# Block 3's cross-attention: groups of two heads by 2048 keys, a lead of three key tiles, first keys loaded beside block 2

## The chip, the cores and the metric

The kernel runs on one core of one Trainium2 chip. The metric is the device time of one execution in microseconds. The program is a four-block perceiver in one launch: each block has a cross-attention to a long context, a self-attention and a feed-forward part, with two batches of 256 query rows and 4096 context rows of 256 values each.

## The reference, cut to what matters

The part that is changed is the cross-attention of block 3: ordinary masked softmax attention of 16 heads of 16 values.

```python
def _L3_xattn_ref(hidden_states, context, attention_mask, q_w, q_b, k_w, k_b, v_w, v_b):
    B, LQ, LK, D = (4, 512, 512, 256)
    H = 16
    HD = D // H
    ...
    q = _split_heads(hidden_states @ q_w.T + q_b)
    k = _split_heads(context @ k_w.T + k_b)
    v = _split_heads(context @ v_w.T + v_b)
    scores = jnp.einsum('bhqd,bhkd->bhqk', q, k) / jnp.sqrt(jnp.float32(HD))
    mask = (attention_mask > 0)[:, None, None, :]
    scores = jnp.where(mask, -jnp.inf, scores)
    probs = jax.nn.softmax(scores, axis=-1)
    ctx = jnp.einsum('bhqk,bhkd->bhqd', probs, v)
    ...
x = x + _L3_xattn_ref(_layernorm(x, axis=-1), ctx_1024, mask_BxS2_ik0, ...)
x = x + _L3_attn_ref(...)
x = x + _L3_ffn_ref(...)
```

In the data x has 2 batches of 256 rows and the context 2 batches of 4096 rows. Block 2 before it ends with a self-attention (`_L2_attn_ref`) and a mixture of eight experts with a shared one (`_L2_ffn_ref`).

## The kernel before, in words

Two "lanes" of tiles, a and x, allocate from the two ends of SBUF and PSUM, so that work of batch 0 and of batch 1, or of two stages, can stand beside each other. Python emits instructions in program order; the framework then places each on its engine's queue by a simulated time line, and each engine runs its queue in order. All loads and stores are issued from SP's queue.

Block 3's keys and values don't depend on x. They are projected earlier, beside blocks 0 to 2 (`prep`, lines 864 to 885), and written to DRAM: keys as a rounded part `kh_d` and its remainder `kl_d`, in units of 512 keys, values as `v_d`, with a column of ones behind each head's 16 values, so that the same product gives the sum of the exponents. `x3_queries` (line 1325) writes the queries of a batch to `q_d` in the same two parts.

`l3_xattn` (line 1333) is a generator; `run` (line 1889) drives it, and where it yields `1, None` the feed-forward part of block 2 for batch 1 (`af(2, 1)`, which is `l2_ffn` and `x3_queries`) is emitted, so that the two run beside each other. The work is cut into groups of four heads (`GRP`), 8 groups in all, and each group into `N_C` = 4 key tiles of 1024 keys: 32 tiles. A key tile `k` is [128, 4 heads, 512]: two halves of 64 partitions, each half 512 keys, and in a half the rows r, r+4, r+8, ... hold the three products of the split (queries high and low against keys high and low), row 3 the mask, row 7 the shift. One contraction over 64 rows so gives the full score, with mask and, later, minus the row's maximum added.

A tile passes twice. `max_steps` (line 1348) loads the tile, multiplies 128 queries by 2 x 512 keys into a tile "f" of two PSUM banks (L1374) and takes maxima on VectorE (L1376), eight steps a tile. When a group's four tiles are through, the maxima are combined (L1380), split in two parts, transposed on PE (`shift_rows`, L557), copied by VectorE (L559) and written by two DMAs into row 7 of the queries. Then `exponents` (line 1385) multiplies again, keys as the stationary operand (L1397), and ScalarE takes exponentials of 128x512 out of a score bank (L1398), two a step, eight steps a tile. `finish` (line 1403) multiplies them by the values (`mh_values`, L580), the four heads of a group in the four 32-row strips of the bank `acc`. At a group's end VectorE copies `acc` (`mh_finish`, L598), PE transposes it (L606), VectorE divides (L609, L610) and POOL adds x and the bias (L1421, L1422).

The maxima run ahead of the exponents by `n_c + LEAD` = 5 tiles. After the first five tiles, `advance` puts one maximum step ahead of each exponent step, and `tie` keeps PE's instructions in that order. Seven key tiles form a ring (`RING`); the rows of ones in them come from a memset by POOL (L1296), once a tile of the ring.

PSUM has eight banks here: two tiles "f" of two banks, one score bank "s" of lane x, two banks "mm" and one "acc" of lane a. Score tiles rotate over "s", "mm", "mm"; the two banks "mm" are also those of block 2's feed-forward part of batch 1, which is emitted first. Small products (L557, L606) take a tile "f". The first four key tiles and the query tiles lie in a pool `early` of lane a; the others in a pool `late` that opens when block 2's attention of batch 1 (`l2_attn(x, 1, ...)`, line 1886) has been emitted.

## Time and profile before

The time is 1528.7 us, median of three executions (1523.4 to 1534.8). The profiled execution took 1525.8 us.

| | PE | DVE | ACT | POOL |
|---|---|---|---|---|
| busy in the span of 1524.0 us | 1363.6 us (89%) | 1109.5 us (73%) | 890.6 us (58%) | 521.0 us (34%) |
| busy from 872 to 960 us | 63.6 | 71.8 | 17.1 | 19.3 |
| busy from 960 to 1241 us | 275.2 | 270.8 | 234.5 | 6.2 |
| busy from 1241 to 1289 us | 46.7 | 3.6 | 43.4 | 1.3 |

In the views of the profile, PE is the matrix engine and PEld its weight loads, DVE is VectorE, ACT ScalarE, POOL GpSimd, SP the engine that issues DMAs; a name with a q is the engine's sequencer. A row of the table of groups gives line, engine, operation, output <- input, shapes and count, then busy time and the mean ns of one, then the idle time of the engine just before these instructions and what ended it. Tile names carry the lane as their first letter: `xf` is the tile "f" of lane x, `amm` a bank "mm" of lane a. A row of a timeline gives start and length in us, engine, line, operation and, in brackets, the idle time before it. PE's busy times are modelled and overlap.

Block 3's cross-attention lies between 872 us, when its first reduction starts, and 1288.6 us, when its last division ends. Block 3's self-attention and experts follow.

### The profile page before, as it was taken

What the parts mean: (1) busy time and instruction counts of PE and PEld (TensorE: products, weight loads), DVE (VectorE), ACT (ScalarE), POOL (GpSimd) and SP (SyncE); (2) the same over time, 40 slices, a digit from 0 to 9 for tenths busy, and PEclk for the clock granted to TensorE, in tenths of its full rate; (3) what the DMA queues carried; (4) which work ended last, traced back from release to release, by engine and by line L of the source; (5) the groups of instructions that cost most, each with busy time, mean ns of one, the idle gap of its engine ahead of it and who ended that gap; (6) DMA issues with size and microseconds to landing.
All of it is one profiled execution on the core that took longest, in us unless ns stands there. A gap on an engine that the chain in (4) does not pass through costs nothing.

```text
span 1524.0 us, 29340 instructions
## 1 busy us (share of the span) xinstructions
PE 1363.6 (89%) x11278; PEld 1117.7 (73%) x11278; DVE 1109.5 (73%) x1879; ACT 890.6 (58%) x1668; POOL 521.0 (34%) x389
## 2 busy tenths in 40 slices
PE   7999888978999999999998677999999999888688
PEld 6898778968998998998897346555555555774587
DVE  6899756437467878885577597899999961575775
ACT  5676555637776655764663312788888897233343
POOL 6755344336355554674235503000000001520230
PEclk9999999979999999999999758899999999996799
DMA  8744064566455566445633642333333312200361
GB/s 295 232 154 134 29 185 156 182 177 200 163 184 175 165 183 210 148 152 176 187 98 102 203 153 79 99 126 117 107 126 106 108 53 66 102 1 3 130 244 56
DMA packets 125143, 212.00 MB, mean 139 GB/s; under 512 B 12840, under 2 KB 89240, under 8 KB 121480
## 3 DMA queue, kind: packets, MB, share of 16 engines
q1 hardware_dynamic: 125004, 210.13, 43.4%
q8 instruction: 89, 1.46, 0.4%
q14 instruction: 50, 0.41, 0.1%
HBM read 181.32 MB, written 28.61 MB: 138 GB/s over the span
## 4 chain that ended last, share of the span: by engine, by line
PE 38%; DVE 24%; DMA 5%; ACT 4%; POOL 4%; issue 3%; SPq 1%; POOLq 0%; DVEq 0%; ACTq 0%
DVE xpm L1376 15%; PE amm L412 9%; PE xmm L412 6%; PE xs L412 4%; PE xpr L412 3%; PE xacc L580 3%; DMA awr<-in_w 2%; PE amm L1397 2%; POOL aw L405 2%; PE xf L1374 1%; PE xmm L784 1%; PE amm L1761 1%; ACT aw L403 1%; PE amm L580 1%; DVE aw L406 1%
## 5 line engine op out<-in xcount | busy, mean ns | idle before, releaser
L1376 DVE TENSOR_REDUCE xpm<-xf 128x2 f32<-128x1024 f32 x256 | 309.8, 1226 | 11.5 <-PE xf L1374 10.1
L1398 ACT ACTIVATE xp<-amm 128x512 f32<-128x512 f32 x342 | 194.5, 595 | 33.7 <-PE amm L1397 16.6
L403 ACT CAST aw<-awr 128x1024 fp32r<-128x1024 f32 (+1 forms) x112 | 114.2, 1021 | 109.8 <-DMA awr<-in_w 55.5
L412 PE MATMUL xmm<-xvx,xpT 128*128 128x256 f32 x1152 | 167.5, 292 | 5.0 <-DVE xpT L787 2.2
L405 POOL TENSOR_TENSOR aw<-awr,aw 128x1024 fp32r<-128x1024 f32 (+1 forms) x53 | 126.2, 2383 | 130.2 <-ACT aw L403 127.8
L412 PE MATMUL xs<-xkx,xqkT 128*128 128x256 f32 x1152 | 163.5, 286 | 1.0 <-ACT xqkT L397 0.6
L734 POOL TENSOR_TENSOR xvx<-xraw,xvx 128x512 fp32r<-128x512 f32 x96 | 132.2, 1392 | 88.8 <-ACT xvx L732 82.9
L580 PE MATMUL xacc<-xp,xv 128*17 128x256 f32 x2048 | 161.1, 387 | 0.9 <-DVE xot L598 0.9
L1374 PE MATMUL xf<-xk,xq 64*128 64x512 f32 x512 | 135.9, 529 | 20.6 <-DVE xpm L1376 13.2
L412 PEld LDWEIGHTS xmm<-xvx,xpT 128*128 128x128 f32 x1152 | 147.9, 193 | 8.6 <-issue 3.6
L412 PEld LDWEIGHTS xs<-xkx,xqkT 128*128 128x128 f32 x1152 | 149.0, 193 | 2.9 <-issue 0.8
L1374 PEld LDWEIGHTS xf<-xk,xq 64*128 64x128 f32 x512 | 51.4, 196 | 125.4 <-issue 86.6
L406 DVE TENSOR_TENSOR aw<-awr,aw 128x1024 fp32r<-128x1024 f32 (+1 forms) x59 | 83.2, 1411 | 64.8 <-ACT aw L403 64.5
L1397 PE MATMUL amm<-xq,xk 64*128 64x256 f32 x684 | 112.5, 294 | 2.7 <-DVE aqT L401 2.6
L1421 POOL TENSOR_TENSOR ax<-ax,ax 128x128 f32<-128x128 f32 x8 | 3.7, 457 | 325.2 <-DVE ax L610 325.2
L1398 ACT ACTIVATE xp<-xs 128x512 f32<-128x512 f32 x170 | 101.1, 595 | 16.5 <-PE amm L1397 11.3
L412 PE MATMUL amm<-axnT,aw 128*128 128x256 f32 x636 | 100.0, 315 | 12.0 <-ACT axnT L403 5.0
L1397 PEld LDWEIGHTS amm<-xq,xk 64*128 64x128 f32 x684 | 95.3, 187 | 17.2 <-issue 12.8
L412 PEld LDWEIGHTS amm<-axnT,aw 128*128 128x128 f32 x636 | 92.0, 219 | 19.8 <-ACT axnT L403 6.8
L412 PE MATMUL amm<-ah,aw 128*128 128x256 f32 x768 | 99.1, 285 | 6.0 <-ACT au L1009 3.1
L734 POOL TENSOR_TENSOR xkx<-xraw,xkx 128x512 fp32r<-128x512 f32 x48 | 73.5, 1531 | 86.6 <-ACT xkx L732 84.2
L412 PEld LDWEIGHTS amm<-ah,aw 128*128 128x128 f32 x768 | 94.3, 190 | 8.5 <-ACT au L1009 3.7
(593 smaller groups left out, 2852.2 us busy)
## 6 DMA issues: line engine op xcount, KB each, us to landing
awr<-in_w SPq DMA_DIRECT2D x105, 512.0 KB
xraw<-in_ctxT SPq DMA_DIRECT2D x108, 256.0 KB
xraw<-in_ctx SPq DMA_DIRECT2D x96, 256.0 KB
xk<-akh_d SPq DMA_DIRECT2D x64, 256.0 KB
av_d<-xkvv SPq DMA_DIRECT2D x16, 544.0 KB
xv<-av_d SPq DMA_DIRECT2D x32, 272.0 KB
akh_d<-xkvk SPq DMA_DIRECT2D x32, 256.0 KB
akl_d<-xkvk SPq DMA_DIRECT2D x32, 256.0 KB
```

Of the source, the lines that this page charges most:

```text
L403: nc.scalar.copy(dst.h, src)
L405: return lo.tensor_tensor(dst.l, src, dst.h.bitcast(F32), ALU.subtract)
L406: return nc.vector.tensor_sub(dst.l, src, dst.h)
L412: tie(self.nc.tensor.matmul(out, lhsT=x, rhs=y, start=start and i == 0, stop=stop and i == 2))
L580: inst = self.nc.tensor.matmul(acc[STRIP * j : STRIP * j + v(j).shape[1], :S], lhsT=v(j), rhs=p[:, j, :], start=start, stop=stop)
L734: nc.gpsimd.tensor_tensor(x.l, r, x.h.bitcast(F32), ALU.subtract)
L784: tie(nc.tensor.transpose(pst[:, t * P : (t + 1) * P], p[:, t * P : (t + 1) * P], self.eye))
L1374: tie(nc.tensor.matmul(both[:, h * 512 : (h + 1) * 512], lhsT=q4[rows, j, t * P : (t + 1) * P], rhs=k4[rows, j, :], start=True, stop=True))
L1376: nc.vector.tensor_reduce(at, both.rearrange("p (h n) -> p h n", h=2), axis=AX.X, op=ALU.max)
L1397: tie(nc.tensor.matmul(ps[h][:, j, :], lhsT=ks[c][rows, a + j, s * P : (s + 1) * P], rhs=q4[rows, a + j, :], start=True, stop=True))
L1398: exps = [nc.scalar.activation(p[:, h, a : a + 2, :], ps[h], AF.Exp, scale=0.25) for h in range(2)]
L1761: nc.tensor.matmul(ps[:, f, :], lhsT=w1[half][:, c, f * P : (f + 1) * P], rhs=buf[:, c, e * cap : (e + 1) * cap], start=c == 0, stop=c == 1)
```

## The change

- A group is two heads (`N_G` = 8 groups a batch), a key tile [128, 2 heads, 1024 keys a half], 2048 keys: `N_C` = 2 tiles a group, still 32 tiles of the same bytes. `prep`, `masks`, `x3_queries` and the DRAM tensors are laid out for it. In `acc` the four strips now hold two heads times two halves of the keys, and a product with two identities on top of each other (`fold`) adds the halves while it transposes.
- The lead is `AHEAD` = 3 tiles, the ring 5, the query sets 4.
- `load_keys` is split from `max_steps`. The loads of the first three tiles are emitted before `next(l3)` returns, ahead of block 2's feed-forward part of batch 1; `early` is now a pool of lane x that opens after the cross-attentions of blocks 0 to 2 have closed theirs, and block 2's attention of batch 1 has weight pools of its own and two instead of four "p" buffers.
- Rows of ones and the mask of the first five tiles come by DMA from a tensor `mo_d`, and the memsets are gone.
- The copy of the shift rows and the copy of `acc` are made by ScalarE.
- PSUM: lane a has one bank "mm", one "s", one "acc". Scores rotate over the two "s", and over "mm" too from tile 4 on (`ALL`). Small products take a score bank instead of a tile "f".

```diff
-    def shift_rows(self, mp, nm, qs, step=1):
+    def shift_rows(self, mp, nm, qs, step=1, copy=None):
...
-            nc.vector.tensor_copy(sh, ps[: 2 * n, :S])
+            (copy or nc.vector.tensor_copy)(sh, ps[: 2 * n, :S])
...
-    def score(self):
+    def score_bank(self):
         self.score_turn = (self.score_turn + 1) % len(self.score_tags)
         lane, tag = self.score_tags[self.score_turn]
-        return lane.t(lane.ps, [P, 512], tag).rearrange("p (a n) -> p a n", a=2)
+        return lane.t(lane.ps, [P, 512], tag)
...
-    N_C = L // 1024
+    N_G, KEYS = HEADS // 2, 1024
+    N_C = L // (2 * KEYS)
...
-    RING = 7
-    Q_SETS = 3
-    LEAD = 1
+    RING = 5
+    Q_SETS = 4
+    ALL = 4
+    AHEAD = N_C + 1
...
-            x = tile(f"k{at}", 512)
-            nc.gpsimd.memset(x.bitcast(F32), 1.0)
-            self.x3_k.append(x)
+            self.x3_k.append(tile(f"k{at}", self.KEYS))
...
+        def load_keys(at):
+            b, g, c, i = place(at)
+            q2, k2 = self.x3_tiles(at)
+            if c == 0:
+                state[i] = q2, k.t(self.early, [P, 2, 2, 4 * n_c], "pm", bufs=2), []
+            g2, u2 = slice(2 * g, 2 * g + 2), slice(2 * c, 2 * c + 2)
+            for r, src in ((0, self.kh_d), (1, self.kh_d), (2, self.kl_d)):
+                nc.sync.dma_start(k2[r :: self.PARTS].bitcast(F32), src[b, u2, :, g2, :].rearrange("u d j n -> (u d) j n"))
+            if at < self.RING:
+                nc.sync.dma_start(k2[self.MASK :: self.PARTS].bitcast(F32), self.mo_d[u2].rearrange("u d j n -> (u d) j n"))
+            else:
+                nc.sync.dma_start(k2[self.MASK :: self.HALF].bitcast(F32), self.mk_d[b, u2])
+            state[i][2].append(k2)
...
+                for r, part in enumerate(k.QUERIES):
+                    src = self.q_d[b, part, :, 2 * g : 2 * g + 2, :].unsqueeze(0).to_broadcast([2, HD, 2, S])
+                    nc.sync.dma_start(q2[r :: self.PARTS].bitcast(F32), src)
...
-            for j in range(GRP):
+            for j in range(2):
                 for t in range(2):
+                    for u in range(2):
+                        both = self.x3_find()
...
-                rest = k.shift_rows(self.early, nm, [(q4, h * self.HALF + self.SHIFT) for h in range(2)], self.PARTS)
+                rest = k.shift_rows(self.early, nm, [(q2, h * self.HALF + self.SHIFT) for h in range(2)], self.PARTS, copy=nc.scalar.copy)
...
-                rest = k.mh_finish(g, acc, out[b])
-                later.append([self.LATER, lambda: finished(rest, b, g)])
+                turn = k.ots[i % 2]
+                nc.scalar.copy(turn, acc[:, :S])
+                later.append([self.LATER, lambda: finished(turn, b, g)])
...
+            ps = k.mm()
+            for t in range(2):
+                tie(nc.tensor.matmul(ps[:, 64 * t : 64 * t + 64], lhsT=oT[:, t * P : (t + 1) * P], rhs=fold, start=True, stop=True))
+            ps = ps[:, :P].rearrange("p (t j r) -> p t j r", t=2, j=2)
+            ri = k.t(k.sm, [P, 2, 2], "x3_ri")
+            nc.vector.reciprocal(ri, ps[:, :, :, HD])
...
-        ahead = n_c + self.LEAD
+        for at in range(self.AHEAD):
+            load_keys(at)
+        yield None
...
-            steps = max_steps(at + ahead) if at + ahead < n else iter(())
-            for s in range(4):
+            if at == self.ALL:
+                k.score_tags.append((self.a, "mm"))
+            if at + self.AHEAD < n:
+                load_keys(at + self.AHEAD)
+                steps = max_steps(at + self.AHEAD)
+            for s in range(0, self.KEYS // P, 2):
...
-        k.mm_from = lambda: self.x3_find()[:, :512]
-        k.score_tags = [(k, "s")] + 2 * [(self.a, "mm")]
+        k.mm_from = k.score_bank
+        k.score_tags = [(k, "s"), (self.a, "s")]
...
-        self.v_d = a.dram([B, 4, P, L // 512, 4 * GRP * (HD + 1)], "v_d")
+        self.v_d = a.dram([B, self.N_G, P, L // P, 2 * (HD + 1)], "v_d")
+        self.mo_d = a.dram([n_u, HD, 2, self.KEYS], "mo_d")
...
-                            if n == 2:
-                                self.early = early.enter_context(a.pool("x3e", bufs=2))
...
-                    x.mm_tags = ["mm", "mm", "pr"]
-                    xb[1] = self.l2_attn(x, 1, xb[1])
+                    self.early = early.enter_context(x.pool("x3e", bufs=2))
+                    with x.pool("wraw", bufs=1) as x.wraw, x.pool("w", bufs=2) as x.wp:
+                        x.mm_tags, x.p_bufs = ["mm", "mm", "pr"], 2
+                        xb[1] = self.l2_attn(x, 1, xb[1])
+                    next(l3)
...
-                with ExitStack() as self.x3_psum, self.psum(a, mm=2, acc=1), x.pool("x3", bufs=2) as self.late:
+                with ExitStack() as self.x3_psum, self.psum(a, mm=1, s=1, acc=1), x.pool("x3", bufs=2) as self.late:
```

## The prediction

> **What bounds the kernel now.** I read the page's table of instruction groups first (which row is largest in block 3), then busy time by stretch around that row, then the timelines of POOL, SP and ScalarE at the two ends of the stage. The first view is the table of groups.
>
> ```profile
> L1376 DVE TENSOR_REDUCE xpm<-xf 128x2 f32<-128x1024 f32 x256 | 309.8, 1226 | 11.5 <-PE xf L1374 10.1
> L1398 ACT ACTIVATE xp<-amm 128x512 f32<-128x512 f32 x342 | 194.5, 595 | 33.7 <-PE amm L1397 16.6
> ```
>
> The maxima of block 3 are 256 reductions of 1.226 us on VectorE, 309.8 us in all, with 11.5 us of idle time before them: 32 key tiles of 8 reductions. The exponents are 342 + 170 = 512 ScalarE rows, 16 a tile. The second view is busy time by stretch (columns: window, length, then PE, PEld, DVE, ACT, POOL busy, granted clock, DMA share, GB/s).
>
> ```profile
> 866.00:872.00 6.00, 0.88 (x4) 0.62 (x4) 5.96 (x4) 0.00 (x0) 6.00 (x7) 0.50 0.83 268
> 872.00:900.00 28.00, 18.47 (x57) 8.28 (x54) 26.86 (x42) 1.28 (x3) 3.15 (x3) 0.50 0.61 205
> 900.00:942.50 42.50, 35.20 (x197) 27.07 (x198) 38.45 (x47) 10.29 (x15) 10.73 (x6) 0.82 0.24 82
> 942.50:960.00 17.50, 9.90 (x48) 8.39 (x48) 6.51 (x14) 5.52 (x7) 5.42 (x3) 0.60 0.27 90
> 960.00:1241.00 281.00, 275.20 (x3033) 146.46 (x3031) 270.76 (x262) 234.50 (x432) 6.21 (x13) 0.99 0.35 110
> 1241.00:1289.00 48.00, 46.68 (x504) 22.75 (x502) 3.57 (x13) 43.39 (x81) 1.25 (x3) 1.00 0.12 34
> ```
>
> The stage has three parts. From 872 to 942.5 us VectorE does the 40 reductions of the five tiles of lead beside block 2's FFN of batch 1, and is busy 65.3 of 70.5 us (0.926). From 942.5 to 960 it has little to do (6.5 of 17.5 us): no exponent has run, since the score banks "mm" of lane a belong to that FFN, and the next reductions come only with exponents. From 960 to 1241 it is the limit (270.8 of 281). From 1241 to 1288.6 reductions are over and ScalarE drains five tiles, 43.4 of 48 us busy. The third view is the timeline of POOL and SP at the start, and of ScalarE and SP where exponents begin.
>
> ```profile
> 868.19 5.28 POOL L1296 MEMSET xk<- 128x2048 f32 x3
> 874.56 0.70 POOL L416 TENSOR_TENSOR abn_rs<-abn_ve,amhalf 128x2 f32<-128x2 f32 x1
> ...
> 911.85 11.91 SPq L340 DMA_DIRECT2D awr<-in_w  x3
> 925.04 1.82 SPq L525 DMA_DIRECT2D xq<-xsh_row  x2
> 933.41 14.84 SPq L340 DMA_DIRECT2D awr<-in_w  x4
> ...
> 1081.46 1.09 ACT L1398 ACTIVATE xp<-amm 128x512 f32<-128x512 f32 x2
> 1082.77 0.60 ACT L1398 ACTIVATE xp<-xs 128x512 f32<-128x512 f32 x1 [0.22 <-PE xs L1397]
> 1083.26 1.26 ACT L1398 ACTIVATE xp<-amm 128x512 f32<-128x512 f32 x2
> ```
>
> POOL's memsets of key tiles stand ahead of the FFN's own power (L416, at 874.56). SP is held 11.9 and 14.8 us at weight loads of the FFN, with the shift rows of group 0 between them.
>
> **What the change leaves as it is.** Tiles stay 32 (16 groups of two heads, two tiles each), with 8 reductions of 128x1024, 32 score matmuls, 16 exponents and the same value matmuls each. Key loads stay 256 KB an issue. So only overlap and small operations differ.
>
> **Term 1, the head.** Now a group is complete after two tiles, 16 reductions instead of 32, and exponents begin after three tiles of lead, in banks that the FFN doesn't hold. I call T4 the moment when tile 4's exponents begin: by then 7 tiles of maxima (56 reductions) and the FFN must be done, since from tile 4 on the bank of lane a is used. The first three key tiles, four loads each, are issued before block 2 ends; the seven memsets (1.79 us each) go, and the ones come by DMA. Before, key loads were issued from 865.6 on and the first reduction began at 872; block 2's attention of batch 1 writes its result at 865.4. So I start at 866. VectorE was busy 79.0 us between 866 and 962; less 41 reductions (50.3) that leaves 28.7 us of FFN and projection. It must now do 56 x 1.226 = 68.7, + 28.7, + two groups' small operations at 1.0 (below) = 99.4 us. At full use T4 is 965; at the 0.926 of the head before it is 866 + 107 = **973**, which I take. Two other limits lie below it. With two score banks a step of exponents costs 0.50 us (score matmul at 1082.27 to exponent at 1082.77 in the timeline) + 1.09 for two exponents = 1.59 us; 32 steps are 51 us; they can start about 893 (16 reductions at 0.926, then some 6 us for transposes, copy and two DMAs), so 944. And the FFN: before, its queries were split at 959.5; POOL frees it 7 us earlier, but lane a now has one bank "mm" instead of two: for ten projections tanh 0.6 + multiply 0.68 + a reduction in front 1.2 = 2.5 us are no longer overlapped, 0 to 25 us, so 952 to 977. I take 965.
>
> **Term 2, the middle.** Before: 27 tiles in 281.0 us, 10.41 each, of which 8 x 1.226 = 9.81; the 2.4 us left over in a group of four tiles are 1.87 us of small VectorE rows (0.22 + 0.17 + 0.17 + 0.40 for the shift, 0.41 copy of acc, 0.21 + 0.29 for the division) and 0.5 idle. After: the two copies (0.40, 0.41) go to ScalarE, the rest, 1.0 us, comes once in two tiles; and the idle 0.5 too, because each group still puts two transposes (0.44 us) and a fold (bounded by the 0.44 of the transposes it replaces) into PE's row, and a small product now takes a score bank until VectorE has divided. So 1.5 us for two tiles, 0.75 a tile: 10.56. Twenty-five tiles from T4 on: **264.0 us**. Bounds: 10.2 if interruptions cost only half their VectorE rows, 11.06 if each group loses 1 us more. ScalarE hides its new copies: 32 exponents x 0.545 = 17.4, + 0.47 (128x256 out of PSUM, nearest row L400) + 0.36 (16x256, a row of L403) = 18.3 of 21.1 us; without that cover they would cost 0.8 us a group, 13 in all, inside the 11.06.
>
> **Term 3, the drain.** Before 47.5 us for 40 steps: 1.12 a step + 2.7 at the end. After 24 steps: 26.9 + 2.7 + 0.9 for two ScalarE copies = **30.5**.
>
> **Sum.** 973 + 264.0 + 30.5 = 1267.5 against 1288.6: 21.1 us less. The profiled execution took 1525.8 us (span 1524.0), 2.9 below the median of the three shown, 1528.7. So **1505**.
>
> **What I set at nothing.** Block 2's attention now loads its weights only after the memory of the third cross-attention is free (805.4), where the split of wk and wv ran at 776: load up to 7 us (twice the 3.5 of a 256 KB key load), cast 1.05, split up to 2.4, issue 0.8, so 816.7; first use was 820.0, behind the layer norm. If the loads queue behind the keys' twelve issues (0.6 us each) it is 4 us late, and so is everything: 0 to 4. Two "p" buffers there instead of four: the reuse lies a group (about 4 us) back, 0. Queries load in three broadcast issues for two heads instead of six for four; shift and zero rows double: SP issues some 5 us in a 10.5 us tile. The values are written in runs of half the length, 16 times, beside transfers that took 0.57 of the DMA time or less: 0. The ones' two extra transfers lie in block 1.
>
> A rule of the skill speaks against the change. The clock in the rows is 0.50 from 866 to 900, where PE was busy 19.4 of 34 us, 0.82 where busy 35.2 of 42.5, 0.99 in the middle. The Trainium skill ("TensorE: Matmul & The Clock Gate", section "A second HAM failure mode: psum-queue depth-cycling") says that PE pausing between groups for PSUM banks can swing the clock between half and full, and two banks in the first four tiles are such a case. At half clock, an estimate by that page, PE's 1.23 us of a step (0.42 of it a gap before weights) would grow to 2.04, 0.45 above the bank cycle, 14 us in 32 steps, and the time would be 1519. The rows say that a fuller PE keeps its clock, and exponents fill PE here, so I add nothing.
>
> **Rivals.** (A) Full packing: VectorE never idles, T4 965, tiles 10.2: 965 + 255 + 29.6 = 1249.6, 39 less: 1487. For it: 0.964 in the middle now; against: the chain of the FFN's router, single small operations each behind a reduction. (B) The toll of smaller groups: tiles of 11.06 (score bank held by the fold, acc held by ScalarE's copy before the next values): 973 + 276.5 + 31 = 1280.5, 8 less: 1518. For: after the fold at 1091.44 the step took 1.96 us instead of 1.23. Against: VectorE itself was used for 0.5 of that.
> (C) Slower: the short lead starves. SP issues in order; behind the FFN's weight loads (held 11.9 and 14.8 us) now stand the shift rows of groups 0 and 1, keys of tiles 5 and 6 and values, which before were in place by 891. PE's scores wait for the shift, and the FFN's own matmuls stand behind them. If exponents so begin only when the FFN ends, at 960, T4 is 960 + 51 = 1011 and the end 1305.5, with 3 us of late weights 1308.5: 20 more, 1546. It decides from T4 = 1288.6 - 294.5 = 994, that is a first exponent later than 943. For it: the held SP rows; against: loads of shift rows are ready to issue between them (925.04), and the head has only 24 reductions to fill.
>
> **How the numbers follow.** Forecast 0.50, own range 1487 to 1524 (T4 963 to 985, tiles 10.3 to 10.8). A 0.12, B 0.18, C 0.20. Range 1483 to 1545: it leaves out some 0.05 below and 0.13 above, in C. One per cent, about what a measurement tells from no change, is 1513.4 to 1544. Faster: 0.46 of the forecast and A = 0.58; within: 0.04 and B, and a little of C = 0.23; slower: 0.19.
>
> **What would show it.** Right: first reduction before 868, first exponents between 890 and 915 in the FFN's stretch, T4 near 973, 84 us per eight tiles afterwards, about 30 us from the last reduction to the end, no memset of xk, block 2's attention still ending near 865. Wrong: idle VectorE between 895 and 960, exponents first after 943, SP rows held over 10 us with xsh_row or xk behind them, "PE waits for ACT or DVE" at L1397 once a group for over 1 us, or a clock below 0.8 in the first four tiles.

## The result, and the profile after

The changed kernel takes 1534.9 us (median of 15 runs, 1524.9 to 1539.3); the kernel before, run beside it on the same chip, 1528.7 (15 runs). The ratio is 1.0043, 95% interval 1.0023 to 1.0064: no faster, some 7 us slower. The profiled execution took 1535.7 us, span 1533.9.

The first view is the table of groups, as shown of the kernel before: the reductions, and two of the three groups of exponents.

```profile
L1398 DVE TENSOR_REDUCE xpm<-xf 128x2 f32<-128x1024 f32 x256 | 309.8, 1222 | 28.8 <-PE xf L1396 27.6
L1422 ACT ACTIVATE xp<-xs 128x512 f32<-128x512 f32 x181 | 107.7, 595 | 25.7 <-PE as L1420 17.3
L1422 ACT ACTIVATE xp<-as 128x512 f32<-128x512 f32 x182 | 108.4, 595 | 24.1 <-PE amm L1420 10.2
```

The reductions cost what they did, but the idle time ahead of them went from 11.5 to 28.8 us, nearly all of it waits for the matrix engine's scores. The second view is busy time by stretch (window, length, PE, PEld, DVE, ACT, POOL, granted clock, DMA share, GB/s): the parts of the stage after, then the whole stage, from the first reduction to the last division.

```profile
882.00:915.00 33.00, 24.39 (x86) 13.27 (x87) 30.90 (x52) 3.09 (x6) 0.69 (x1) 0.55 0.39 133
915.00:960.00 45.00, 41.84 (x344) 29.09 (x342) 33.15 (x38) 25.81 (x45) 12.18 (x7) 1.00 0.29 88
960.00:1001.00 41.00, 37.48 (x271) 18.53 (x268) 27.75 (x34) 22.77 (x42) 4.21 (x5) 0.79 0.46 145
1001.00:1269.00 268.00, 263.74 (x2885) 139.71 (x2877) 253.21 (x270) 224.66 (x427) 9.04 (x27) 1.00 0.36 108
1269.00:1300.00 31.00, 29.55 (x315) 14.82 (x316) 1.73 (x8) 27.24 (x52) 0.98 (x4) 1.00 0.11 27
...
882.00:1300.00 418.00, 397.00 (x3887) 215.44 (x3888) 346.73 (x398) 303.58 (x569) 27.11 (x44) 0.94 0.34 106
```

The same row of the kernel before:

```profile
872.00:1289.00 417.00, 385.46 (x3828) 212.94 (x3826) 346.15 (x374) 294.98 (x537) 26.77 (x28) 0.92 0.33 104
```

**The stage is as long as it was**, 417.7 us against 416.6, and it starts 10 us later. VectorE does the same work in it; the matrix engine does 11.5 us more and is busy for 397 of 418 us. The points on the way, in us:

| | before | after | forecast |
|---|---|---|---|
| third cross-attention of batch 1 written | 806.3 | 809.6 | |
| block 2's attention of batch 1 written | 865.4 | 880.6 | near 865 |
| first reduction | 872.0 | 882.1 | 866 |
| first exponent | 960.1 | 915.8 | 893 |
| block 2's FFN of batch 1 written | 948.5 | 958.9 | 952 to 977, with queries |
| T4, scores of tile 4 begin | | 1001.5 | 973 |
| last reduction ends | 1241.0 | 1269.4 | 1237 |
| last division ends | 1288.6 | 1299.8 | 1267.5 |

The drain (last reduction to last division) shrank from 47.6 to 30.4 us, as forecast; the head swallowed it. Before, 88 us lay ahead of the first exponent and 328.5 behind it. Now it is 33.7 and 384.0. The 54 us won ahead of it were lost behind it: the first 32 steps of exponents, beside the FFN, took 85.7 us, 2.7 each, where a step in the middle takes 1.34. The rest of the loss, the later start, lies in block 2's attention: 71.0 us from the third cross-attention to its result, 59.1 before. Third view: SP's timeline near the attention's end, in the kernel before and then in the changed one. L525 are the stacks, the loads that put a group's queries and keys into their rows; the last row is the matrix engine's, the first scores of the last group.

```profile
846.36 1.36 SPq L525 DMA_DIRECT2D xq<-xa2q  x3
847.77 0.29 SPq L525 DMA_DIRECT2D xq<-xa2s  x1
848.10 0.25 SPq L525 DMA_DIRECT2D xk<-xa2s  x1
848.45 0.84 SPq L340 DMA_DIRECT2D awr<-in_w  x2
850.73 0.38 SPq L520 DMA_DIRECT2D aq_d<-aqT  x1
```

```profile
858.84 0.90 SPq L525 DMA_DIRECT2D xq<-xa2q  x2
860.98 1.54 SPq L1345 DMA_DIRECT2D aq_d<-aqT  x2
862.57 0.46 SPq L525 DMA_DIRECT2D xq<-xa2q  x1
863.08 0.28 SPq L525 DMA_DIRECT2D xq<-xa2s  x1
863.95 0.58 SPq L1345 DMA_DIRECT2D aq_d<-aqT  x1
864.57 0.44 SPq L525 DMA_DIRECT2D xk<-xa2s  x1
...
867.05 0.71 PE L573 MATMUL xs<-xq,xk 128*128 128x256 f32 x4 [0.51 <-DMA xk<-xa2s]
```

L1345 is new: block 3's queries of batch 0 go out in four stores, one for each half of the heads and each part, where it was one (L520). Each waits for its part of aqT, which ScalarE (high part) and VectorE (low part) make, and the last group's stacks of batch 1's attention stand between and behind them on SP. That group's scores start at 867.05 and have waited for the last of these stacks; they lie 6.1 us behind those of the group before it, in the kernel before (851.5) 3.6. The queries of batch 1 go out in four stores too, from 977.4 to 981.8, inside the stage.

### The profile page after: what moved, and what is told of

It reads as the page before. It is cut to its first block, busy times and chain, and to the rows that moved or that the text cites. A ratio compares the mean times of both kernels' runs of the same rounds, so it can differ in the third digit from the quotient of the medians.

```text
span 1533.9 us, 29631 instructions
## 1 busy us (share of the span) xinstructions
PE 1383.0 (90%) x11342; PEld 1123.7 (73%) x11342; DVE 1105.4 (72%) x1904; ACT 899.6 (59%) x1700; POOL 511.8 (33%) x399
## 4 chain that ended last, share of the span: by engine, by line
PE 51%; DVE 10%; DMA 7%; ACT 6%; POOL 3%; issue 3%; SPq 1%; POOLq 0%; DVEq 0%; ACTq 0%
PE xacc L580 8%; PE amm L412 8%; PE xf L1396 6%; PE xmm L412 6%; PE xs L412 4%; DMA awr<-in_w 4%; PE xpr L412 3%; DVE xpm L1398 2%; PE xs L1420 2%; PE as L1420 2%; ACT xp L1422 1%; PE amm L1420 1%; POOL aw L405 1%; PE xmm L787 1%; PE amm L1803 1%
## 5 line engine op out<-in xcount | busy, mean ns | idle before, releaser
L1398 DVE TENSOR_REDUCE xpm<-xf 128x2 f32<-128x1024 f32 x256 | 309.8, 1222 | 28.8 <-PE xf L1396 27.6
L1396 PE MATMUL xf<-xk,xq 64*128 64x512 f32 x512 | 135.1, 526 | 12.0 <-DVE xpm L1398 11.2
L1422 ACT ACTIVATE xp<-xs 128x512 f32<-128x512 f32 x181 | 107.7, 595 | 25.7 <-PE as L1420 17.3
L1422 ACT ACTIVATE xp<-as 128x512 f32<-128x512 f32 x182 | 108.4, 595 | 24.1 <-PE amm L1420 10.2
L1456 POOL TENSOR_TENSOR ax<-ax,ax 128x64 f32<-128x64 f32 x16 | 5.1, 321 | 299.1 <-DVE ax L1455 299.1
L1422 ACT ACTIVATE xp<-amm 128x512 f32<-128x512 f32 x149 | 88.7, 595 | 13.4 <-PE xs L1420 10.1
L776 ACT ACTIVATE xp<-xs,xnm 128x512 f32<-128x512 f32 x96 | 66.3, 690 | 35.5 <-DVE xnm L770 33.3
```

Source lines behind the costliest of these rows:

```text
L776: tie(nc.scalar.activation(p, score.pop(i), AF.Exp, bias=least[q], accum_out=su))
L1396: tie(nc.tensor.matmul(both[:, h * 512 : (h + 1) * 512], lhsT=q2[rows, j, t * P : (t + 1) * P], rhs=k2[rows, j, at], start=True, stop=True))
L1398: nc.vector.tensor_reduce(at, both.rearrange("p (h n) -> p h n", h=2), axis=AX.X, op=ALU.max)
L1422: after = nc.scalar.activation(p[:, a, h], ps[h], AF.Exp, scale=0.25)
```

## The experiments

Each edit is to the changed kernel unless it says otherwise. "Head" is first reduction to T4 (119.4 us in the changed kernel), "stretch" the third cross-attention to block 2's attention (71.0; 59.1 before). Ratios are to the kernel before, run beside it (1524.9 to 1526.0 us), with 95% intervals. One traced execution places a point to some 5 us (the third cross-attention ended between 802 and 815 in kernels that do the same up to there), so differences within one trace are read, not clock times across traces. The 15 runs of the changed kernel spread over 14 us, so where only one execution was taken its time says little, and its trace is read instead.

**Why block 2's attention is late.** First, the key loads emitted behind the yield:

```diff
-        for at in range(self.AHEAD):
-            load_keys(at)
         yield None
...
         for at in range(self.AHEAD):
+            load_keys(at)
             steps = max_steps(at)
```

> The changed kernel, with the key loads, the query tiles and the rows of ones of the first three tiles emitted behind the yield, tile by tile ahead of their maximum steps, as the kernel before had it; all else as changed. Theory 1 (the preload delays block 2's attention of batch 1: two casts on POOL stand ahead of its layer norm, twelve issues on SP ahead of its stacks): the attention's result, at 880.6 us in the changed kernel, comes back by 8 to 15 us (866 to 873); the first reduction then lies some 6 us behind it instead of 1.5, so the time falls by 3 to 9 us, to 1526 to 1532. Rival (the attention is late because its weights load late and its p buffers are two, whatever the keys do): the result stays at 878 to 882, the first reduction moves back to about 886, and the time grows by some 5 us, to 1540.

1533.3 us, ratio 1.0047 (1.0027 to 1.0067); stretch 71.3, first reduction 1.6 us behind. Nothing moved, the loads included: they are still issued from 809 on, since the queue is ordered by simulated readiness, and the memory of `early` is free then. Neither theory was tested. Next, the memory of the kernel before:

```diff
+                                if n == 2:
+                                    self.early = early.enter_context(a.pool("x3e", bufs=2))
                                 xb[1] = self.xattn(xp, n, 1, xb[1], xq[1])
...
-                    self.early = early.enter_context(x.pool("x3e", bufs=2))
-                    with x.pool("wraw", bufs=1) as x.wraw, x.pool("w", bufs=2) as x.wp:
-                        x.mm_tags, x.p_bufs = ["mm", "mm", "pr"], 2
-                        xb[1] = self.l2_attn(x, 1, xb[1])
+                    x.mm_tags = ["mm", "mm", "pr"]
+                    xb[1] = self.l2_attn(x, 1, xb[1])
```

> The changed kernel, with the memory of the kernel before around block 2's attention of batch 1: its weights come from the pools of lane x that stand open from the start, it has four p buffers, and the pool of the first keys is one of lane a, opened before the third cross-attention of batch 1; key loads stay emitted before the feed-forward part. Theory (the attention is late because its weight loads wait for the memory of the cross-attention, and its two p buffers and the keys crowd into the same stretch): result of the attention at 866 to 872 instead of 880.6, everything behind it earlier by 9 to 14, time 1521 to 1526. Rival (the four stores of the queries and the key issues on SP are what delays it): the result stays within 4 us of 880, the time within 4 us of 1535.

1530.1 us, 1.0027 (1.0004 to 1.0051); stretch 64.8, but the keys, whose memory was that of block 2's FFN of batch 0, were issued only from 861, and the first reduction lay 4.1 us behind the attention. By the ratios that is 2 us less than the changed kernel, which the intervals do not tell from nothing; 9 to 14 were expected. Then early weights with the keys left early (weight pools open to the end, four p buffers), and the same with the queries in one store, as in the kernel before:

```diff
+            with x.pool("wraw", bufs=1) as x.wraw, x.pool("w", bufs=2) as wp, ExitStack() as early:
...
-                    with x.pool("wraw", bufs=1) as x.wraw, x.pool("w", bufs=2) as x.wp:
-                        x.mm_tags, x.p_bufs = ["mm", "mm", "pr"], 2
+                    x.mm_tags, x.p_bufs = ["mm", "mm", "pr"], 4
```

```diff
-            for m in range(2):
-                for r in range(2):
-                    dst = self.q_d[b, r, :, HEADS // 2 * m : HEADS // 2 * (m + 1), :].rearrange("d h n -> h d n")
-                    self.nc.sync.dma_start(dst, qT.both[:, r, m, :].bitcast(F32))
+            k.to_dram(k.proj_t_split(wq, xnT, ap, "qT", bias="x3.bq"), self.q_d[b])
```

> The changed kernel; the weight pools of lane x stay open from the start until block 3's cross-attention is done, so that block 2's attention of batch 1 loads its weights early as in the kernel before, and it has four p buffers; the keys of the first three tiles are still issued beside it, and the queries still go out in four stores. The stretch from the end of the third cross-attention to the end of that attention was 59 us in the kernel before, 71 in the changed one, 65 with the old pools (weights early, four p buffers, keys late). Theory (late weights and the p buffers cost 6 of the 12, the preload nothing): 64 to 66 us, first reduction 1 to 2 us later, so T4 and the end 6 us earlier, time 1526 to 1531. Rival (the preload costs them, and the old pools gained by losing it): 69 to 71 us, time 1533 to 1537.

> As the run with early weights and four p buffers, and the queries of a batch go out in one store in the layout of the kernel before, to be loaded in six issues a group instead of three. Theory (the four stores, which wait on SP for ScalarE's aqT, hold back the last groups' stacks and cost the other 4 to 6 of the 12 us): attention's stretch 59 to 61, time 4 to 6 us below the run with four stores, 1521 to 1526. Rival (three more issues a group on SP, 0.6 us each, hold keys and shift rows back in the head and in the middle): stretch shorter, but tiles of 11 us or a T4 no earlier, time not below the run with four stores.

Early weights: 1534.1 us, 1.0063 (1.0041 to 1.0086), stretch 66.8: shorter by 4, and no time won. With one store: 1524.0 us, 0.9990 (0.9960 to 1.0019), stretch 63.4. The one store is worth 10 us, more than expected, though a group's queries then take six loads instead of three. So it was undone alone, and, the other way round, the four were kept and issued by POOL, with early weights:

```diff
-                    self.nc.sync.dma_start(dst, qT.both[:, r, m, :].bitcast(F32))
+                    self.nc.gpsimd.dma_start(dst, qT.both[:, r, m, :].bitcast(F32))
```

> The changed kernel with one part undone: the queries of a batch go out in one store and come back in six loads a group, as in the kernel before; weights late, two p buffers, three key tiles early, all as changed. Early weights and four p buffers alone left the time where it was (1534.1), the same with one store gave 1524.0. Theory (the four stores on SP are the whole loss): 1523 to 1527. Rival (they hurt only where the weights are early, or the late weights then show): 1529 to 1533.

> The kernel with early weights and four p buffers (1534.1 us), with the four stores of the queries issued by POOL instead of SP, so that nothing on SP waits for ScalarE's aqT, while a group's queries still load in three issues. Theory (the stores hold back the stacks behind them on SP): at least the gain of the single store, since three issues a group are saved as well: 1519 to 1524. Rival (the gain of the single store lies in its one large transfer, or POOL is held by its own issues): 1525 to 1534.

One store alone: 1525.1 us, ratio 1.0000 (0.9978 to 1.0022). Four stores off SP: 1525.4, 0.9988 (0.9966 to 1.0011). **The loss is the four stores in SP's queue**: undone in either way, nothing is left of it that the intervals show (some 3 us to either side), weights early or late. How they cost it shows in the pair that differs in the issuing engine alone. Early weights with four stores on SP, SP's rows and the last group's first scores:

```profile
853.35 1.36 SPq L525 DMA_DIRECT2D xq<-xa2q  x3
855.66 3.27 SPq L1345 DMA_DIRECT2D aq_d<-aqT  x4
858.98 0.45 SPq L525 DMA_DIRECT2D xq<-xa2s  x1
859.49 0.26 SPq L525 DMA_DIRECT2D xk<-xa2s  x1
...
862.15 0.71 PE L573 MATMUL xs<-xq,xk 128*128 128x256 f32 x4 [0.40 <-DMA xk<-xa2s]
```

With the same stores on POOL:

```profile
858.25 1.36 SPq L525 DMA_DIRECT2D xq<-xa2q  x3
859.65 0.28 SPq L525 DMA_DIRECT2D xq<-xa2s  x1
859.98 0.25 SPq L525 DMA_DIRECT2D xk<-xa2s  x1
```

The stores hold SP for 3.3 us amid the last group's stacks, and its scores start 6.5 us behind the third group's; with the stores on POOL it is 3.2, and no scores wait for a stack. The SP timeline with the one store alone:

```profile
856.26 1.36 SPq L525 DMA_DIRECT2D xq<-xa2q  x3
857.66 0.28 SPq L525 DMA_DIRECT2D xq<-xa2s  x1
857.99 0.25 SPq L525 DMA_DIRECT2D xk<-xa2s  x1
858.34 4.27 SPq L340 DMA_DIRECT2D awr<-in_w  x2
862.70 0.38 SPq L520 DMA_DIRECT2D aq_d<-aqT  x1
```

The last group's stacks are out before the store, and from the attention's first scores to its last it now takes 20.9 us, where the changed kernel took 24.3 and the kernel before 15.8. So some 2 to 3 us of the 7 to 10 are seen here. In the trace of one store alone, stretch and head together are 6.4 us shorter than in the changed kernel (67.2 and 116.8 us), all that the ratios show; between early weights and the same with stores by POOL it is only 2.4 (66.3 and 116.5 us against 66.8 and 118.4). All these edits undo the stores of both batches, so what batch 1's cost in the head is not told apart. The stretch is still 67 us against 59. Is the rest the preload? Only the first tile early, and query tiles filled by ScalarE, on top of early weights and one store:

```diff
-            return k.t(self.early if at < self.AHEAD else self.late, ...)
+            return k.t(self.early if at < 1 else self.late, ...)
-            nc.gpsimd.tensor_copy(x, self.unmask.unsqueeze(1).to_broadcast([P, 2, S]))
+            nc.scalar.copy(x, self.unmask.unsqueeze(1).to_broadcast([P, 2, S]))
```

> The kernel with early weights and one store of the queries (1524.0 us), with only the first key tile and the first query tile loaded beside block 2's attention instead of three and two; tiles two and three load when the attention has freed its memory, and the query tiles are filled by ScalarE instead of POOL (0.6 us instead of 1.2). Theory (what is left of the attention's delay, a stretch of 63 us against 59, is the preload: two casts of POOL ahead of the layer norm, eight key issues among SP's weight loads): stretch 59 to 61, first reduction still 1.5 to 3 us behind it, tile two in place in time since the first takes 10 us: time 2 to 4 us less, 1520 to 1522. Rival (the delay is noise of the stretch, or the later tiles come late behind the feed-forward part's weight loads): no gain, 1523 to 1528.

1526.8 us, 1.0012 (0.9991 to 1.0032). The stretch is 60.2 us, as the theory had it, the first reduction 1.1 us behind, and yet no time is won, as the rival had it: 3 us of stretch in one trace don't reach the median, here or with early weights alone. Where they go stays open.

**What sets the head and the middle.** A lead of five tiles (the first three still early):

```diff
-    RING = 5
-    AHEAD = N_C + 1
+    RING = 7
+    AHEAD = N_C + 3
```

> The changed kernel with a lead of five tiles and a ring of seven; the first three tiles are preloaded as in the changed kernel, the next two load behind. Theory of the prediction (VectorE sets the head): sixteen more reductions, 19.6 us, before the first exponent and the same later; T4 (first exponents of the fifth tile) rises from 1001 by about 20, the middle has two tiles less (-21.4), the drain grows by 17 to about 47: the time grows by 15 to 18 us, to 1550 to 1553. Theory now (the matrix engine sets the head, since exponents and their values stand beside the feed-forward part's matmuls; VectorE idles meanwhile): reductions in place of exponents fill VectorE in that stretch, the feed-forward part ends 5 to 10 us earlier, T4 rises by only 3 to 8 us, and the time changes by -3 to +4.

1539.6 us, 1.0091 (1.0057 to 1.0124). T4 at 1014.1, 135.6 us behind the first reduction: 16 more. T4 is nearer the first theory: of 19.6 us of reductions 16 showed, and the FFN ended no earlier (959.4). The time, some 7 us above the changed kernel's by the ratios, lies between the two. Then the matrix work of that FFN cut to a third:

```diff
         for i, (x, y) in enumerate(((a.h, b.h), (a.h, b.l), (a.l, b.h))):
+            if i and self.top.one_part:
+                break
```

> The changed kernel; in block 2's feed-forward part of batch 1 each split product computes only its first of three matmuls (the two with the low parts are left out), so that its matrix work falls to a third; its loads, casts, VectorE, ScalarE and POOL instructions stay. T4 is the start of the fifth tile's exponents, 1001.3 in the changed kernel. Theory now (the matrix engine sets the head): some 170 matmuls of 0.14 us at full clock, twice that at half, fewer up to T4, so T4 falls by 15 to 25 us, to 976 to 986. Theory of the prediction (VectorE sets it) or the rival that the chain of weight loads on SP sets it: T4 falls by less than 5 us.

One execution, 1523.2 us; head 111.3, 8 less, FFN done at 946.6 instead of 958.9. Less than expected, and the rows say why: the matrix engine is just as full, at half the clock, until 943.

```profile
920.00:925.00 5.00, 5.00 (x29) 2.80 (x29) 2.53 (x4) 3.51 (x6) 3.60 (x2) 0.50 0.14 17
925.00:930.00 5.00, 5.00 (x29) 2.58 (x21) 4.12 (x5) 3.12 (x7) 0.72 (x1) 0.50 0.40 142
```

In the changed kernel the clock was 1.00 from 915 to 960. So the cut neither shows that the matrix engine sets the head nor rules it out. Then VectorE's work cut:

```diff
-    nc.vector.tensor_reduce(at, both.rearrange("p (h n) -> p h n", h=2), axis=AX.X, op=ALU.max)
+    nc.vector.tensor_reduce(at, both.rearrange("p (h n) -> p h n", h=2)[:, :, :256], axis=AX.X, op=ALU.max)
```

> The changed kernel; each reduction takes the maximum over half of the columns (128x512 instead of 128x1024), so half of the scores are left out of the maximum; the matrix engine's and ScalarE's work stays. A reduction then takes some 0.68 us (the 128x512 row of L406) instead of 1.22. T4 (first exponents of the fifth tile) is 1001.3 in the changed kernel, its 25 tiles in the middle take 10.72 each. Theory of the prediction (VectorE sets head and middle): T4 about 30 us earlier, tiles of 9.0 to 9.2 (the 1.12 us a step of the drain), some 65 to 75 us less in all. Theory now (the matrix engine has as much to do and is full from the first exponent on): T4 earlier by at most 12, through the reductions ahead of the first exponent alone, tiles of 10.0 to 10.6, 10 to 30 us less in all.

One execution, 1514.2 us. Busy time in head, middle and drain:

```profile
882.00:987.00 105.00, 98.12 (x702) 59.12 (x702) 65.02 (x122) 52.36 (x93) 17.21 (x13) 0.86 0.42 137
987.00:1252.00 265.00, 262.50 (x2875) 139.68 (x2872) 148.86 (x269) 223.59 (x425) 9.08 (x27) 1.00 0.35 110
1252.00:1283.00 31.00, 29.94 (x322) 14.88 (x314) 1.42 (x7) 27.69 (x53) 0.85 (x3) 1.00 0.10 24
```

VectorE's work in the stage falls from 346.7 to 215.3 us; the head is 14.5 shorter (7.5 of it ahead of the first exponent), the middle 2.5: tiles of 10.62 instead of 10.72. **VectorE alone sets neither**: of the 30 us that the prediction's theory wanted in the head about half showed, and in the middle VectorE is busy for 149 of 265 us and the pace stays. The matrix engine's timeline of the changed kernel in the middle shows a second thing of the same length:

```profile
1101.77 0.63 PE L580 MATMUL xacc<-xp,xv 128*17 128x256 f32 x8
1102.32 0.50 PE L1396 MATMUL xf<-xk,xq 64*128 64x512 f32 x2
1102.66 0.28 PE L1420 MATMUL as<-xq,xk 64*128 64x256 f32 x1
1102.66 0.39 PE L1420 MATMUL amm<-xq,xk 64*128 64x256 f32 x2
1102.78 0.27 PE L1420 MATMUL as<-xq,xk 64*128 64x256 f32 x1
1102.98 0.63 PE L580 MATMUL xacc<-xp,xv 128*17 128x256 f32 x8
```

Values, maxima, scores and the next values, one behind the other with no wait: a step of 1.21 us, beside a reduction of 1.22. Two attempts to cut it:

> The changed kernel; of the four value products of a score tile in block 3's cross-attention only two are computed (the first half of the keys; the other half of the values is left out), so the matrix engine has some 0.3 us less in each step of 1.3; VectorE, ScalarE and the loads stay. Theory now (the matrix engine is full from the first exponent on): T4 8 to 14 us earlier than 1001.3, tiles down from 10.72 to the 10.1 to 10.3 that VectorE needs, drain down to the 1.09 a step of ScalarE, 18 to 28 us less in all. Theory of the prediction (VectorE sets head and middle, ScalarE the drain): T4 and tiles within 3 us and 0.15 of what they were, 0 to 7 us less in all.

One execution, 1531.4 us; tiles of 10.66, head 119.6, nothing gained. The edit did not cut what it was meant to: eight products of a step take 0.63 us, the four that are left 0.61, as if the four strips ran beside each other.

```diff
+            if s not in (1, 3, 5, 6):
                 k.mh_values(p, lambda j: v[:, j // 2, s, j % 2, :], acc, c + s == 0, end, after, tie)
```

> The changed kernel; in every second step of block 3's cross-attention all eight value products are left out (half of the keys' values are not summed), which takes 0.28 us a step on average off the matrix engine, whose step of scores, values and maxima starts every 1.22 us; VectorE and ScalarE stay. Theory P (the matrix engine alone sets the middle and the head behind the first exponent): tiles of 8.7 to 9.2, T4 10 us earlier, 45 to 55 us less. Theory P and V (matrix step and VectorE's reduction are both 1.22 us, so neither cut alone helps in the middle): tiles of 10.0 to 10.5, drain down to ScalarE's 1.09 a step, T4 5 to 12 us earlier by the head, where VectorE has slack: 10 to 25 us less. Theory V (VectorE alone): less than 8 us less.

> The changed kernel with both cuts: maxima over half of the columns and the value products of every second step left out. Half maxima alone gave tiles of 10.62. Theory P and V: now both are out of the way and ScalarE's 16 exponents a tile (8.7) or the drain's 1.1 a step set the pace: tiles of 8.8 to 9.5, 50 to 80 us less than the changed kernel. If something else sets the middle (score banks that wait for exponents, transfers of keys), tiles stay above 10.

1543.0 and 1537.4 us, one execution each: with less work the stage is no shorter, 433 and 420 us against 417.7. The mean clock fell to 0.910 and 0.917 (0.936 in the changed kernel). Where it stayed at 1.00, between 1040 and 1120 us, 80 us hold 124 exponents in both runs and 122 in the changed kernel and with half maxima: tiles of 10.3 against 10.5. With both cuts the matrix engine is busy for 70.4 of these 80 us, VectorE for 43.9 and ScalarE for 69.4, and the pace hardly rises, so something else holds it. The matrix engine now waits for exponents to free a score bank:

```profile
1061.31 0.38 PE L1420 MATMUL as<-xq,xk 64*128 64x256 f32 x1 [0.33 <-ACT xp L1422]
...
1063.71 0.38 PE L1420 MATMUL amm<-xq,xk 64*128 64x256 f32 x1 [0.34 <-ACT xp L1422]
```

Two steps in 2.40 us, 1.20 each with three banks. That the three banks are this third limit is argued from these waits; what a fourth would give was not tried. Of the theories on the three cuts none held; only the last sentence on both cuts did, that tiles stay above 10.

**The copies and the small products.** The copies back on VectorE, and, in the kernel before, on ScalarE:

```diff
-                rest = k.shift_rows(..., self.PARTS, copy=nc.scalar.copy)
+                rest = k.shift_rows(..., self.PARTS)
...
-                nc.scalar.copy(turn, acc[:, :S])
+                nc.vector.tensor_copy(turn, acc[:, :S])
```

> The changed kernel with the two copies of a group (shift rows and acc) made by VectorE again, 0.40 and 0.41 us. Theory of the prediction (VectorE sets the middle): 25 tiles are 12.5 groups, 0.81 us each: the middle grows by 10 us, the time by 9 to 12, to 1544 to 1547. Rival (in groups of two heads the matrix engine is as full as VectorE, so the copies fit into waits for scores): the time grows by 0 to 4.

> The kernel before with one part of the change alone: the copies of the shift rows and of acc in block 3's cross-attention are made by ScalarE. Theory of the prediction (VectorE sets the middle: 270.8 of 281 us): 6.75 groups of 0.81 us come off it, -5.5 us, and the drain grows by under 1: time 1520 to 1523 where the kernel before has 1525.6. Rival (the copies now stand in ScalarE's row behind exponents, and scores or the next group's values wait for them, or the matrix engine is at its limit itself): -2 to +3.

Copies by VectorE again: 1533.4 us, 1.0052 (1.0031 to 1.0073), as the changed kernel. Copies by ScalarE in the kernel before: 1525.1, 0.9983 (0.9957 to 1.0009). The first is the rival's: the 9 to 12 us are ruled out. Its trace shows part of them all the same: from T4 to the last reduction 273.3 us instead of 267.9, but a head of 115.1 instead of 119.4. The interval of the second (6.6 us less to 1.4 more) holds both theories; in its trace the time from first exponent to last reduction is 281.8 us, 280.9 before, so nothing was won there. Next, the kernel with early weights and one store, with the small products in a tile f:

```diff
-        k.mm_from = k.score_bank
+        k.mm_from = lambda: self.x3_find()[:, :512]
```

> The kernel with early weights and one store of the queries (1524.0 us), with the small products of a group (transposes of the shift rows, fold) in a two-bank tile f again, as in the kernel before, instead of a score bank. Theory A (a score bank held until VectorE has divided costs each group an exponent step, 0.3 to 0.6 us): middle down from 10.67 to 10.4 a tile, 4 to 8 us less. Theory B (a held tile f delays the reductions, which are as tight): middle 10.7 to 11.0, 1 to 8 us more.

1534.3 us, 1.0057 (1.0035 to 1.0079), against 1524.0 without the edit: a tile f for transposes and fold costs 10 us, theory B; from T4 to the last reduction 274.1 us instead of 266.8. This part of the change helps, so it was put into the kernel before (`k.mm_from = k.score_bank` there), alone and with the copies:

> The kernel before with one part of the change alone: transposes of the shift rows and of acc take a score bank instead of a two-bank tile f. With sixteen groups this was worth 10 us. Theory (the toll is per group: a held tile f stops the reductions): eight groups, 3 to 6 us less, 1519 to 1522. Rival (in the kernel before two of three score banks are those of the feed-forward part in the head, and the shift of group 0 then waits there): no gain or a loss, 1524 to 1530.

> As the run with the kernel before and small products in a score bank, with the copies of shift rows and acc by ScalarE as well. Theory (the matrix engine's step and VectorE's reduction are equal, so the copies alone gave 0.9 us, but with tile f free they count): 1 to 4 us less than without the copies, 1517 to 1521. Rival (the matrix engine's step sets the pace all the same): within 2 us of the run without them.

**1516.1 us, ratio 0.9944 (0.9921 to 0.9967)** alone, 1516.4, 0.9950 (0.9932 to 0.9968) with the copies: the fastest version of the study, and faster than both kernels. The copies add nothing, as the rival had it. The gain is somewhat more than expected, and the trace doesn't show where: its stage is 415.9 us long against 416.6, and the 7 us between the two traced executions lie behind it, where traces of other kernels differ by as much (227 to 237 us). Where the gain lies stays open.

## Why the prediction was wrong

The stage ended 32.3 us behind the forecast: 16.1 by its start, 12.4 by the head, 3.9 by the middle and -0.1 by the drain.

- **Start, 866 forecast, 882.1 measured.** The failing step is "what I set at nothing": I priced the weights (0 to 4 us), the p buffers (0) and the loads of the queries, and left out the stores. The diff replaces one store by four, with a wait for ScalarE, ahead of the last stacks of the attention that starts everything; with them undone the time is that of the kernel before, 7 to 10 us less. One row of SP's queue before, L520 at 850.73 in front of the weight loads, was enough to ask what stands behind four. The stores are not all of the 16 us: with one store the first reduction still came at 878.2, and what holds the stretch at 67 us instead of 59 is not settled. The 5 us that I expected between attention and first reduction were won: 1.5 us instead of 6.6.
- **Term 1, 107 us forecast from the start to T4, 119.4 measured.** I summed VectorE and divided by its use of the head before. This step failed as well: from 915 to 1001 VectorE was busy for 60.9 of 86 us and the matrix engine for 79.3, and with half of the reduction time cut about half of the forecast gain came. Reductions alone left the matrix engine room for the FFN (63.6 of 88 us busy between 872 and 960, a row I had); exponents, at 1.21 us of matrix time a step, leave little. That the matrix engine sets the head instead is argued from these rows: with the FFN's products cut to a third the head fell by 8 us only, at half clock. The stores alone do not explain the miss: without them the kernel is still at 1525, not at 1505.
- **Term 2, 264.0 forecast, 267.9 measured**, 10.72 a tile, inside my bounds. The size was nearly right by luck, the reason was not: I called VectorE the limit at 270.8 of 281 us, and the same row has the matrix engine at 275.2. The copies that I took off VectorE would have cost 5 us there by one trace, not the 10 of my sum, and nothing in the whole; and the place of the small products, which I charged with 0.5 us of idle time a group either way, is worth 10 us.
- **Term 3, 30.5 forecast, 30.4 measured.** But it was no gain. In the drain before, the matrix engine was busy for 46.7 of 48 us: the steps that left it had to be paid elsewhere. As an estimate, the whole stage could give the matrix engine's idle time in it, 417 - 385 = 32 us, as long as its clock stays as it is, and in the changed kernel that engine is busy for 11.5 us more.
- **Rivals.** The time lies between B (1518) and C (1546), but neither mechanism is what happened: tiles were 10.72, not 11.06, and exponents began at 915.8, not 960. C's break-even points the right way: T4 lay 7 us behind its 994 and the middle took 4 us longer than forecast, so the stage ended 11.2 us later than before in the two traces, where the ratio says some 7.
- **The clock.** I added nothing. From 915 to 960 it was 1.00, from 960 to 1001 0.79. The trace shows what a short wait does: ScalarE's cast of a weight waits 1.45 us for its load, exponents stand behind it, and the matrix engine behind them.

```profile
958.00:961.00 3.00, 2.90 (x28) 1.34 (x27) 3.00 (x6) 1.14 (x3) 0.00 (x0) 1.00 0.77 244
961.00:964.00 3.00, 1.47 (x10) 0.82 (x12) 3.00 (x5) 2.26 (x4) 1.81 (x1) 0.80 0.28 113
964.00:970.00 6.00, 6.00 (x37) 2.34 (x32) 3.65 (x5) 2.98 (x6) 1.23 (x2) 0.50 0.44 140
970.00:976.00 6.00, 6.00 (x32) 3.71 (x29) 3.14 (x3) 2.09 (x5) 0.00 (x0) 0.50 0.57 155
```

Three microseconds half empty, then twelve at half clock, in which a step with no other products between takes 2.1 us instead of 1.6. The Trainium skill ("TensorE: Matmul & The Clock Gate", section "A second HAM failure mode: psum-queue depth-cycling") says that frequent short idle times of the matrix engine between groups, as it cycles through PSUM banks, make its clock swing. These rows agree in kind: a wait of 1.51 us for a score bank lies ahead of the half clock. My estimate by that page had been 1519; what the swing cost no run shows.

## What to carry to other kernels

Before a drain or a lead is shortened, read the row of busy time of the engine that is fullest over the whole stage, the parts to be shortened included: its idle time is a first estimate of what overlap can give. Where several limits of a step are equal (here 1.22, 1.21 and perhaps 1.20 us), cutting one alone was worth 2.5 us in the middle, or nothing. And count the DMA issues that a new layout adds to a queue that runs in order, with what each waits for and who stands behind it: four stores in place of one, for each batch, made the difference between no gain and a loss.

## What the runs showed of the hardware

Less matrix work need not be faster. With the values of every second step left out, the matrix engine was busy for 32.25 of 36 us at full clock, and after a stretch with 5.84 of 8 it was at half (one traced execution):

```profile
1100.00:1136.00 36.00, 32.25 (x296) 17.59 (x294) 34.32 (x36) 31.95 (x61) 0.64 (x2) 1.00 0.40 121
1136.00:1144.00 8.00, 5.84 (x54) 3.21 (x50) 7.04 (x15) 5.80 (x12) 1.37 (x3) 0.94 0.43 143
1144.00:1160.00 16.00, 15.56 (x90) 8.07 (x88) 10.95 (x12) 9.64 (x19) 0.00 (x0) 0.50 0.22 67
```

Its drain, too, ran at a mean clock of 0.63 (1.00 in the changed kernel). And products of 17 columns in four strips cost no more than in two: 0.63 and 0.61 us.
